# Where the constant rows of a decoder's running sums are written, and the order of four of its stages

## The chip, the cores and the metric

The kernel runs on one core of a Trainium2 chip, as one program and one launch. Its time is the device time of one execution in microseconds (us). The core has five engines that run independently: TensorE (PE, with its weight loads shown as PEld), VectorE (DVE), ScalarE (ACT), GpSimd (POOL) and SyncE (SP, which only issues transfers). Transfers (DMAs) are issued by SP, ACT and POOL and are moved by 16 DMA engines.

## What is computed

The reference is a decoder of four layers over 16 sequences of 128 tokens, 256 wide, in fp32. Each layer has an attention, a cross attention and a feed-forward part, every one followed by `x = _layernorm(x + part(x))`, so there are twelve stages in a chain, called s0 to s11 here. The change touches five of them:

- s0, a gated delta-rule attention. Its decays are products over time, computed as exponentials of differences of running sums.
- s3, a retention attention. Queries and keys are turned by position: `x * c + _rot(x) * s`, where `_rot` swaps neighbouring features. Then the scores `Q K^T` are multiplied with a decay matrix, and the output is normalised and gated.
- s1 and s2, a cross attention and a feed-forward part that is a table of splines, whose end is worked through together.
- s5, a gated feed-forward part with integer weights: `down(silu(gate(x)) * up(x))`, 704 hidden columns.
- s9, a state space layer (Mamba2) with 64 heads. The lines that matter:

```python
dt = jax.nn.softplus(dt + dt_bias)
A = -jnp.exp(A_log)
dA = jnp.transpose((dt * A).reshape(B_, nc, CS, NH), (0, 3, 1, 2))
A_cum = jnp.cumsum(dA, axis=-1)
Lmat = jnp.exp(_segsum(dA))
```

`_segsum` is the difference of two running sums for each pair of times.

## The kernel before, in words

The 16 sequences are worked as four groups (NG = 4) of four. `X` (tokens by features) and `xT` (its transpose) stay in SBUF for the whole run. A stage ends for a group with `finish_in_turns` (line 487): moments, normalisation, transposes into `xT`.

**Order of the work.** Stages are written as generators, and functions such as `rota` (line 290) take one step of each in turn. Where `self.nc` is an `Ordered` (line 320), compute instructions stay on their engine in the order in which they are written; nearly all instructions pass through there, so the profile shows them under line 332. Transfers on SP and parts that are not `Ordered` are placed by the framework's scheduler.

**Running sums (s0, s9).** The differences of running sums come out of a small matmul, 30 rows deep, whose two operands lie in one tile `up`. Its rows hold the sums, split in three parts and each part in a high and a low half, and constant rows of ones and selections. `sums` (line 402) makes DRAM tiles whose rows are filled from the constants, four heads at a time: it issues four transfers from DRAM to DRAM on ACT's queue, 256 KB each for s0 (`starts`) and 1024 KB each for s9 (`sums`). The kernel then overwrites the rows of the sums (for s0 at lines 663 and 664), and `load_sums` (line 413) reads a unit's rows into its `up`. s0's `sums` is called at line 594 in `w0`; s9's in `w7`, but it depends on nothing and is placed at the start of the run.

**The start.** SP loads `X`, `wab`, `w`, `sl`, `tbl` and the first weights, ACT loads constants. PE transposes `X` (line 476), ACT copies the transposes into `xT` (line 479). Slopes (`ss`, line 1097 and 1098) come from `sl`, and the gates of s0 from `wab`; from these come the sums `cums`, and with them stage s0 begins.

**s12_late** (line 1192) is the end of s1 and s2 with the first steps of s4's keys beside it. `s2_scores` marks for each token its bin (`oh`), and `turn(g)` transposes a group's marks on PE. All turns but the last come before the last call of `s2_scores`.

**s3.** `s3_turned` (line 1339) makes one half of a group's queries or keys: two projections, a copy `raw`, a transfer that swaps neighbouring rows (`sw`), two multiplications (`t` on POOL, `sw` on DVE) and their addition, on POOL. For keys ACT then writes two scaled copies `k`. `s3_unit` does the scores, decay (`ret` on DVE), normalisation (`var`, a power on POOL) and gating of a sequence.

**s5.** `s5_groups` (line 1828) goes through the groups one after the other: 48 matmuls for gate and up with ACT and DVE in between, then 48 matmuls for the down product, then `finish` of the group. The last group's `finish` is left to s6 (line 1911), where `first.insert(1, self.finish_in_turns(NG - 1))` puts it beside the first latents. In s4, `s5_prepare` (line 1778) prepares the integer weights step by step.

**s9.** Before its loop, `s9_sums` (line 2479) makes `dt`, `dA` and the sums of all four groups: 32 matmuls, softplus as Exp and Ln on ACT, the split in three parts on DVE, 48 matmuls with a triangle of ones, 24 transfers. `s9_group(0)` (line 2528) makes B and C of group 0. Then 64 units run (`s9_unit`, line 2564; four groups of 16), one step of each of the last units in every round of `rota`. A unit loads `wzx`, has 16 matmuls of 512 columns, 8 transposes (`xs`), 4 difference matmuls, 32 small ones (`y`) and 8 output matmuls (bankC). At its first step it takes one step of `more`; for units 8 to 15 of a group that is the next group's `s9_group`, for units 0 to 7 it is empty.

Of the kernel before, what the change touches and what calls it, by code (L numbers as in the profile page):

```python
# [22 lines left out]
S = 128  # L23
D = 256
NG = 4
# [309 lines left out]
class Decoder:  # L335
# [66 lines left out]
    def sums(self, heads, name):  # L402

        tiles = [self.dram.tile([heads, 32, S], F32, name=f"{name}_{g}") for g in range(NG)]
        lo = self.at["consts"]["up9"][0]
        for t in tiles:
            self.nc.scalar.dma_start(
                t.rearrange("(q i) r t -> q (i r) t", i=4),
                self.a["consts"][:, lo : lo + 128].unsqueeze(0).to_broadcast([heads // 4, 128, S]),
            )  # L410
        return tiles
# [173 lines left out]
    def w0(self, pool):  # L585
        nc = self.nc
        w = {}
        w["tri_le"] = self.const(pool, "tri_le", nc.scalar)
        w["tri_s"] = self.const(pool, "tri_s", nc.scalar)
        w["levels"] = self.const(pool, "levels", nc.scalar)  # L590
        w["ident32"] = self.const(pool, "ident32", nc.scalar)
        w["wab"] = pool.tile([128, 2, 32], F32, name="wab")
        nc.sync.dma_start(w["wab"], self.a["s0_wab"].rearrange("(k p) c -> p k c", p=128))
        self.starts0 = self.sums(16, "starts0")
        self.ends0 = [self.dram.tile([4, 16, 6, S], F32, name=f"ends0_{g}") for g in range(NG)]
        return w
# [595 lines left out]
    def s12_late(self, k12, wk, w, held, last):  # L1192
# [19 lines left out]
        for g in range(NG - 1):  # L1212
            turn(g)
        for _ in self.s2_scores(k12, held, NG - 1):
            next(keys, None)
        turn(NG - 1)
# [122 lines left out]
    def s3_turned(self, wk, w, g, part, qk):  # L1339
# [24 lines left out]
        if m == 0:  # L1364
            nc.gpsimd.tensor_tensor(q[:, c], t, sw, ALU.add)
        else:
            nc.gpsimd.tensor_tensor(t, t, sw, ALU.add)
            for par in range(2):
                nc.scalar.activation(kk[:, c, par], t, AF.Copy, scale=self.parity[:, par : par + 1])
# [391 lines left out]
    def w5(self, pool):  # L1761
# [10 lines left out]
        w["wide"] = pool.tile([128, 1], I32, name="wide5")  # L1772
        w["first"] = [
# [4 lines left out]
    def s5_prepare(self, w):  # L1778

        nc = self.nc  # L1780
        gur, wdr = w["gur"], w["wdr"]
        for k in range(2):
            for m in range(2):
                nc.gpsimd.tensor_scalar(gur[:, k, m, :704], w["gu_i"][:, k, m], 128.0, None, ALU.subtract)
                yield
# [42 lines left out]
    def s5_groups(self, wk, w, halves, last):  # L1828
# [12 lines left out]
        for g in range(NG):  # L1841
            if halves:
                hs = [wk.tile([128, 6, 512], F32R, tag="h5" + "hl"[n], name="h5" + "hl"[n]) for n in pair]
                gu, wd, xs = w["gur"], w["wdr"], halves[g]
            else:
                hs = [wk.tile([128, 6, 512], F32, tag="h5h", name="h5")]
                gu, wd, xs = w["gu"], w["wd"], [self.xT[:, :, 512 * g : 512 * g + 512]]
            of = len(xs)
            for c in range(6):
                n = 128 if c < 5 else 64  # L1850
                cols = slice(128 * c, 128 * c + (128 if halves else n))
                ps = []
                for m in pair:
                    p = self.ps(512)
                    for k in pair:
                        for i, x in enumerate(xs):
                            lhsT = gu[:, k, m, cols]
                            self.mm(p[: lhsT.shape[-1]], lhsT, x[:, k, :], of * k + i, 2 * of)
                    ps.append(p)
                t = wk.tile([128, 512], F32, tag="t5", name="t5")  # L1860
                nc.scalar.activation(t[:n], ps[0][:n], AF.Silu, scale=self.col("s5_sg")[:n, c : c + 1])
                h = wk.tile([128, 512], F32, tag="hf5", name="hf5", bufs=3) if halves else hs[0][:, c, :]
                nc.vector.scalar_tensor_tensor(
                    h[:n], ps[1][:n], self.col("s5_su")[:n, c : c + 1], t[:n], ALU.mult, ALU.mult
                )
                if halves:
                    nc.scalar.copy(hs[0][:n, c, :], h[:n])
                    nc.gpsimd.tensor_tensor(hs[1][:n, c, :], h[:n], hs[0][:n, c, :].bitcast(F32), ALU.subtract)
            if g == 0:
                self.load_transposed(NG - 1)  # L1870
            if halves and g + 2 < NG:
                halves.append(self.s5_halves(wk, g + 2))
            for half in pair:
                p = self.pt(2, D)
                for j in pair:
                    for c in range(6):
                        n = 128 if c < 5 else 64
                        lo = (2 * half + j) * 128
                        for i, h in enumerate(hs):
                            self.mm(p[:, j, :], h[:n, c, lo : lo + 128], wd[:n, c, :], of * c + i, of * 6)  # L1880
                t = wk.tile([128, 2, D], F32, tag="y5", name="y5")
                nc.vector.tensor_tensor(t, p, bc(self.row("s5_sd").unsqueeze(1), 128, 2, D), ALU.mult)
                xs_ = self.X[:, 4 * g + 2 * half : 4 * g + 2 * half + 2, :]
                nc.gpsimd.tensor_tensor(xs_, xs_, t, ALU.add)
            if last or g + 1 < NG:
                self.finish(g, last)

# [5 lines left out]
    def w6(self, pool):  # L1893
# [12 lines left out]
        w["vo"] = pool.tile([128, 8, D], F32, name="wvo6")  # L1906
        for t, src in zip((w["q"][:, :, 0, :], w["q2"][:64], w["vo"]), self.absorbed):
# [3 lines left out]
    def s6(self, wk, w, last):  # L1911
# [11 lines left out]
        first.insert(1, self.finish_in_turns(NG - 1))  # L1923
# [212 lines left out]
    def w7(self, pool):  # L2136
        self.sums9 = self.sums(64, "sums9")
# [309 lines left out]
    def s9(self, wk, w, last):  # L2447
# [12 lines left out]
        with (  # L2460
# [18 lines left out]
    def s9_sums(self, wk, w):  # L2479

        nc, pair = self.nc, range(2)
        dts = [w["dt"][:, 8 * k : 8 * k + 8, :] for k in pair]

        def twice(tag, bufs):
            return [wk.tile([128, 8, 64], F32, tag=tag, name=tag, bufs=bufs) for _ in pair]

        ea = wk.tile([128, 64], F32, tag="th9", name="ea9")
        nc.scalar.activation(ea, self.row("s9_al"), AF.Exp)
        for g in range(NG):
            gs = slice(4 * g, 4 * g + 4)  # L2490
            p = self.ps(4, 64)
            for j in range(4):
                for k in range(2):
                    self.mm(p[:, j, :], self.xTs(k, 4 * g + j), w["bcd"][:, k, 256:320], k, 2)
            nc.vector.tensor_tensor(
                w["dt"][:, gs, :], p, bc(self.row("s9_dtb").unsqueeze(1), 128, 4, 64), ALU.add
            )
        da = twice("sz9", 5)
        for d, t in zip(da, dts):
            nc.vector.scalar_tensor_tensor(d, t, -1.0, t, ALU.mult, ALU.min)  # L2500
        for d in da:
            nc.scalar.activation(d, d, AF.Exp)
        for d in da:
            nc.scalar.activation(d, d, AF.Ln, bias=1.0)
        parts = [twice("yx9", 2), twice("gT9", 2), da]
        for k in pair:
            d, t = da[k], dts[k]
            nc.vector.scalar_tensor_tensor(t, t, 0.0, d, ALU.max, ALU.add)
            nc.vector.scalar_tensor_tensor(d, t, -1.0, bc(ea.unsqueeze(1), 128, 8, 64), ALU.mult, ALU.mult)
        for n, unit in enumerate((2.0**-4, 2.0**-16)):  # L2510
            big = MAGIC * unit
            for k in pair:
                nc.vector.tensor_scalar(parts[n][k], da[k], big, big, ALU.add, ALU.subtract)
                nc.vector.tensor_tensor(da[k], da[k], parts[n][k], ALU.subtract)
        for g in range(2):
            for n in range(3):
                p = self.ps(4, 128)
                for j in range(4):
                    for k in pair:
                        self.mm(p[64 * k : 64 * k + 64, j, :], parts[n][k][:, 4 * g + j, :], w["tri_le"])  # L2520
                both = [wk.tile([128, 4, S], F32R, tag="m9", name="sum9", bufs=8) for _ in pair]
                self.halves(*both, p)
                for k in pair:
                    for hl in pair:
                        rows = self.sums9[2 * k + g][:, 10 * n + 5 * hl : 10 * n + 5 * hl + 4]
                        (nc.scalar, nc.gpsimd)[k].dma_start(rows, both[hl][64 * k : 64 * k + 64].bitcast(F32))
# [299 lines left out]
```

## Time and profile before

Three executions took 3757.82 us (median; 3754.70 and 3765.27 the others). The profile is of one more execution.

| | |
|---|---|
| the profiled execution's own time | 3764.13 us |
| its span, from the first to the last instruction | 3762.4 us |
| mean granted TensorE clock | 0.956 |
| PE busy | 3422.7 us, 91% of the span |
| DVE, ACT, POOL busy | 68%, 56%, 53% |

By time from the start of the span, the stages that matter lie so:

| stretch (us) | work | length (us) | PE busy (us) |
|---|---|---|---|
| 0 to 61 | start, gates and sums of s0 | 61 | 22.0 |
| 1387 to 1488 | s12_late | 101 | 74.4 |
| 1488 to 1640 | s3 | 152 | 126.8 |
| 1808 to 1905 | s5 | 97 | 86.4 |
| 2536 to 2607 | s9 ahead of its steady loop | 71 | 55.6 |
| 2607 to 3510 | the loop of s9 | 903 | 878.0 (some records are missing) |

In a line of the timeline the columns are: start, duration, engine, source line, operation, result and operands, their partitions and elements, how many of them; in brackets the engine's idle time before and what ended it. In a line of waits they are: the instruction that waited and its line, what it waited for; then the sum of the waits in us, how many, and the longest. Windows give per stretch the busy time of each engine (with the number of instructions), then the granted PE clock and the share and rate of the DMA engines.

### The profile page before, as it was taken

What the parts mean: (1) busy time and instruction counts of PE and PEld (TensorE: products, weight loads), DVE (VectorE), ACT (ScalarE), POOL (GpSimd) and SP (SyncE); (2) the same over time, 40 slices, a digit from 0 to 9 for tenths busy, and PEclk for the clock granted to TensorE, in tenths of its full rate; (3) what the DMA queues carried; (4) which work ended last, traced back from release to release, by engine and by line L of the source; (5) the groups of instructions that cost most, each with busy time, mean ns of one, the idle gap of its engine ahead of it and who ended that gap; (6) DMA issues with size and microseconds to landing.
All of it is one profiled execution on the core that took longest, in us unless ns stands there. A gap on an engine that the chain in (4) does not pass through costs nothing.

```text
span 3762.4 us, 95159 instructions
## 1 busy us (share of the span) xinstructions
PE 3422.7 (91%) x38821; PEld 2127.4 (57%) x38821; DVE 2547.4 (68%) x5495; ACT 2114.5 (56%) x4682; POOL 2012.6 (53%) x2313
## 2 busy tenths in 40 slices
PE   4899999999999987878889999988999999999896
PEld 3566666666666655656646665665455554555453
DVE  2677777767877756568444557756777777777797
ACT  2566666666666634345435445535666665666386
POOL 2344444444443434764455542345887676777467
PEclk8999999999999987978999998998999999999898
DMA  5111111111111115031100003112111111111220
GB/s 156 32 42 39 40 36 40 39 35 40 39 37 35 32 67 207 35 115 45 36 27 29 26 34 102 46 56 82 47 43 47 43 45 44 44 47 40 74 75 25
DMA packets 145271, 199.50 MB, mean 53 GB/s; under 512 B 14816, under 2 KB 98656, under 8 KB 141248
## 3 DMA queue, kind: packets, MB, share of 16 engines
q1 hardware_dynamic: 128912, 180.06, 14.9%
q10 hardware_dynamic: 14672, 9.03, 0.9%
q8 instruction: 310, 5.08, 0.5%
q0 software_dynamic: 1248, 4.28, 0.4%
q14 instruction: 129, 1.06, 0.1%
HBM read 159.49 MB, written 26.48 MB: 49 GB/s over the span
## 4 chain that ended last, share of the span: by engine, by line
PE 41%; DVE 9%; ACT 2%; POOL 2%; issue 2%; DMA 1%; SPq 0%; ACTq 0%; POOLq 0%; DVEq 0%
PE bankA L332 18%; PE bankB L332 15%; PE bankC L332 6%; DVE npad L332 2%; PE bankA L511 1%; PE bankB L511 1%; DVE y L332 1%; DVE acc L332 1%; DVE t L332 1%; DVE h L332 0%; DVE xp L332 0%; DVE X L332 0%; ACT L332 0%; DVE ln_st L332 0%; ACT e L332 0%
## 5 line engine op out<-in xcount | busy, mean ns | idle before, releaser
L332 PE MATMUL bankA<-xT,wzx 128*128 128x512 f32 x1024 | 458.5, 601 | 0.1
L332 DVE SCALAR_TENSOR_TENSOR acc<-bankA,half,acc 128x508 f32<-128x508 f32 (+2 forms) x384 | 285.3, 743 | 167.5 <-ACT acc L332 158.5
L332 PEld LDWEIGHTS bankA<-xT,wzx 128*128 128x128 f32 x1024 | 190.5, 191 | 226.4 <-issue 187.9
L332 POOL TENSOR_TENSOR m<-m,gm 128x512 f32<-128x512 f32 x252 | 312.8, 1275 | 9.8 <-ACT m L332 9.8
L332 PE MATMUL bankA<-xT,wkq 128*128 128x512 f32 x512 | 254.5, 621 | 0.4 <-ACT eb L332 0.2
L332 PE MATMUL bankA<-xT,wvg 128*128 128x512 f32 x512 | 251.7, 615 | 0.5 <-issue 0.5
L332 POOL TENSOR_TENSOR gT<-yx,sz 128x512 f32<-128x512 f32 x126 | 158.0, 1275 | 174.3 <-DVE yx L332 174.0
L332 POOL TENSOR_TENSOR eb<-eb,c_tri_s 128x512 f32<-128x512 f32 x64 | 81.2, 1268 | 299.2 <-ACT eb L332 299.2
L332 PE MATMUL bankC<-gT,wo 128*128 128x512 f32 x512 | 230.4, 593 | 1.5 <-DVE gT L332 1.5
L332 DVE TENSOR_REDUCE npad<-bankA 128x2 f32<-128x512 f32 (+1 forms) x320 | 197.2, 682 | 36.7 <-PE bankA L332 36.3
L332 ACT ACTIVATE m<-bankA 128x512 f32<-128x512 f32 x256 | 132.0, 603 | 129.2 <-PE bankA L332 129.2
L332 ACT ACTIVATE e<-bankA 128x512 f32<-128x512 f32 x320 | 164.9, 602 | 67.4 <-PE bankA L332 66.6
L332 POOL TENSOR_SCALAR rs_ve<-o_mv 128x4 f32<-128x4 f32 x64 | 31.6, 493 | 303.2 <-DVE o_mv L332 292.3
L332 POOL TENSOR_TENSOR sq<-sq,s 128x512 f32<-128x512 f32 x124 | 158.1, 1275 | 59.5 <-ACT s L332 54.8
L332 DVE SCALAR_TENSOR_TENSOR vT<-th,accv 128x512 f32<-128x512 f32 x64 | 45.8, 716 | 185.1 <-ACT th L332 185.1
L332 PEld LDWEIGHTS bankB<-y,tt 32*32 32x32 f32 x8192 | 86.8, 106 | 110.2 <-issue 76.2
L332 DVE SCALAR_TENSOR_TENSOR acck<-bankA,half_cols,acck 128x508 f32<-128x508 f32 (+2 forms) x192 | 142.5, 742 | 8.2 <-ACT acck L332 1.7
L332 PEld LDWEIGHTS bankC<-gT,wo 128*128 128x128 f32 x512 | 92.9, 190 | 96.4 <-issue 93.2
L332 ACT ACTIVATE acc<-bankA,half 128x512 f32<-128x512 f32 x128 | 100.6, 786 | 81.0 <-PE bankA L332 76.0
L332 DVE SCALAR_TENSOR_TENSOR accq<-bankA,half_cols,accq 128x508 f32<-128x508 f32 (+2 forms) x192 | 142.2, 741 | 4.5
L332 DVE SCALAR_TENSOR_TENSOR accv<-bankA,half_cols,accv 128x508 f32<-128x508 f32 (+2 forms) x192 | 140.1, 730 | 4.5
L332 ACT ACTIVATE m<-m 128x512 f32<-128x512 f32 x256 | 141.2, 650 | 0.0
(523 smaller groups left out, 9354.2 us busy)
## 6 DMA issues: line engine op xcount, KB each, us to landing
wzx<-in_s_wzx SPq DMA_DIRECT2D x64, 512.0 KB
wkq<-in_s_w SPq DMA_DIRECT2D x64, 256.0 KB
wvg<-in_s_w SPq DMA_DIRECT2D x64, 256.0 KB
wo<-in_s_wo SPq DMA_DIRECT2D x64, 128.0 KB
keys<-k SPq DMA_DIRECT2D x8, 1024.0 KB
k<-keys SPq DMA_DIRECT2D x8, 1024.0 KB
eo<-in_ctx_eo SPq DMA_DIRECT2D x32, 256.0 KB
e<-in_ctx_e SPq DMA_DIRECT2D x32, 256.0 KB
```

Of the source, the lines that this page charges most:

```text
L332: return lambda *a, **k: self.tc.keep_in_program_order(f(*a, **k))
L511: self.nc.tensor.matmul(out, lhsT=lhsT, rhs=rhs, start=(k == 0), stop=(k == n - 1))
```

## The change

It has these parts.

- `sums` writes its four tiles from a pattern in SBUF that `sums_first` loads (64 KB), and does so on SP. For s0 the pattern is loaded behind `wab`, and the four writes stand on SP behind `w` and ahead of `sl`, `tbl` and the first weights. For s9 the pattern is loaded in `w5` and the four writes are the first step of `s5_prepare`, during s4.
- In `s12_late` the turn of group 2 moves into the last call of `s2_scores`, behind its fourth step.
- In `s3_turned` the addition goes from POOL to DVE, for queries and for keys.
- `s5_groups` is cut in `s5_gates` and `s5_down`: the next group's gates stand ahead of a group's down product, and a group's `finish` is taken in two parts, the second behind the gates after that. The rest of the last `finish` goes to s6 as `self.ends`.
- `s9_sums` works for one group. Group 0's runs step by step beside `s9_group(0)` ahead of the loop, now in program order; those of groups 1 to 3 are steps of `more` for units 0 to 5 of the group before. Exp of `A_log` is taken once, ahead of it.

```diff
-    def sums(self, heads, name):
+    def sums_first(self, pool):
+        lo = self.at["consts"]["up9"][0]
+        first = pool.tile([128, 128], F32, name="sums_first")
+        self.nc.sync.dma_start(first, self.a["consts"][:, lo : lo + 128])
+        return first
+
+    def sums(self, first, heads, name):
         tiles = [self.dram.tile([heads, 32, S], F32, name=f"{name}_{g}") for g in range(NG)]
-        lo = self.at["consts"]["up9"][0]
         for t in tiles:
-            self.nc.scalar.dma_start(
-                t.rearrange("(q i) r t -> q (i r) t", i=4),
-                self.a["consts"][:, lo : lo + 128].unsqueeze(0).to_broadcast([heads // 4, 128, S]),
+            self.nc.sync.dma_start(
+                t.rearrange("(q i) r t -> (i r) q t", i=4), bc(first.unsqueeze(1), 128, heads // 4, 128)
             )
         return tiles
...
-        self.starts0 = self.sums(16, "starts0")
+        self.starts0 = self.sums(self.sums_first(pool), 16, "starts0")
...
-        for g in range(NG - 1):
+        for g in range(NG - 2):
             turn(g)
-        for _ in self.s2_scores(k12, held, NG - 1):
+        for n, _ in enumerate(self.s2_scores(k12, held, NG - 1)):
             next(keys, None)
+            if n == 3:
+                turn(NG - 2)
         turn(NG - 1)
...
-            nc.gpsimd.tensor_tensor(q[:, c], t, sw, ALU.add)
+            nc.vector.tensor_tensor(q[:, c], t, sw, ALU.add)
         else:
-            nc.gpsimd.tensor_tensor(t, t, sw, ALU.add)
+            nc.vector.tensor_tensor(t, t, sw, ALU.add)
...
+        w["sums"] = self.sums_first(pool)
...
+        self.sums9 = self.sums(w["sums"], 64, "sums9")
...
+        turned = {}
+        for g in range(NG + 1):
+            if g < NG:
+                turned[g] = self.s5_gates(wk, w, halves, g)
+                if g == 0:
+                    self.load_transposed(NG - 1)
             if halves and g + 2 < NG:
                 halves.append(self.s5_halves(wk, g + 2))
+            if g > 1:
+                for _ in ends:
+                    pass
+            if g:
+                self.s5_down(wk, w, halves, g - 1, turned.pop(g - 1))
+                ends = self.finish_in_turns(g - 1, last)
+                if last or g < NG:
+                    next(ends)
+        if last:
+            for _ in ends:
+                pass
+        else:
+            self.ends = [ends]
...
-        first.insert(1, self.finish_in_turns(NG - 1))
+        first.insert(1, self.ends[0])
...
-        self.sums9 = self.sums(64, "sums9")
...
-            self.s9_sums(wu, w)
-            for _ in self.s9_group(wu, w, 0):
+            ea = w["ea"] = wk.tile([128, 64], F32, name="ea9", **one)
+            nc.scalar.activation(ea, self.row("s9_al"), AF.Exp)
+            self.nc = Ordered(self.tc, nc)
+            for both in zip_longest(self.s9_sums(wu, w, 0), self.s9_group(wu, w, 0)):
                 pass
-            self.nc = Ordered(self.tc, nc)
...
-                    more, held = iter(()), {}
+                    more, held = self.s9_sums(wu, w, u // 16 + 1) if u < 48 else iter(()), {}
...
+    def s9_sums(self, wk, w, g):
+        nc = self.nc
+        t = w["dt"][:, 4 * g : 4 * g + 4, :]
+        d, part = [wk.tile([128, 4, 64], F32, tag=n, name=n, bufs=1) for n in ("da9", "part9")]
+        p = self.ps(4, 64)
+        for j in range(4):
+            for k in range(2):
+                self.mm(p[:, j, :], self.xTs(k, 4 * g + j), w["bcd"][:, k, 256:320], k, 2)
+        nc.vector.tensor_tensor(t, p, bc(self.row("s9_dtb").unsqueeze(1), 128, 4, 64), ALU.add)
+        nc.vector.scalar_tensor_tensor(d, t, -1.0, t, ALU.mult, ALU.min)
+        yield
+        nc.scalar.activation(d, d, AF.Exp)
+        nc.scalar.activation(d, d, AF.Ln, bias=1.0)
+        yield
+        nc.vector.scalar_tensor_tensor(t, t, 0.0, d, ALU.max, ALU.add)
+        nc.vector.scalar_tensor_tensor(d, t, -1.0, bc(w["ea"].unsqueeze(1), 128, 4, 64), ALU.mult, ALU.mult)
+        yield
+        for n in range(3):
+            src = d
+            if n < 2:
+                src, big = part, MAGIC * (2.0**-4, 2.0**-16)[n]
+                nc.vector.tensor_scalar(part, d, big, big, ALU.add, ALU.subtract)
+                nc.vector.tensor_tensor(d, d, part, ALU.subtract)
+            p = self.ps(4, 128)[:64]
             for j in range(4):
+                self.mm(p[:, j, :], src[:, j, :], w["tri_le"])
+            both = [wk.tile([64, 4, S], F32R, tag=f"sum9{m}", name="sum9", bufs=1) for m in range(2)]
+            self.halves(*both, p)
+            for m in range(2):
+                rows = self.sums9[g][:, 10 * n + 5 * m : 10 * n + 5 * m + 4]
+                nc.scalar.dma_start(rows, both[m].bitcast(F32))
+            yield
```

The bodies of `s5_gates` and `s5_down` are the two halves of the old `s5_groups`, unchanged. `w6` wraps its `nc` in `Ordered` ahead of three loads on SP, which `Ordered` passes through as they are.

More of the change, by code (lines that the diff above doesn't have):

```diff
@@ L1840, in s5_groups @@
             nc.gpsimd.tensor_scalar(wd[:64, 5, :], w["d_i"][:64, 5, :], 128.0, None, ALU.subtract)
[L1841 to L1870, printed above, removed]
@@ L1871, in s5_groups @@
+        turned = {}
[4 more added lines that the diff above has]
+                    self.load_transposed(NG - 1)
             if halves and g + 2 < NG:
                 halves.append(self.s5_halves(wk, g + 2))
[L1873 to L1884, printed above, removed]
@@ L1885, in s5_groups, with s5_operands @@
-            if last or g + 1 < NG:
-                self.finish(g, last)
+            if g > 1:
[11 more added lines that the diff above has]
+            self.ends = [ends]
+    def s5_operands(self, w, halves, g):
+        if halves:
+            return w["gur"], w["wdr"], halves[g]
+        return w["gu"], w["wd"], [self.xT[:, :, 512 * g : 512 * g + 512]]
@@ new lines, in s5_gates @@
+    def s5_gates(self, wk, w, halves, g):
+        nc = self.nc
+        pair = range(2)
+        if halves:
+            hs = [wk.tile([128, 6, 512], F32R, tag="h5" + "hl"[n], name="h5" + "hl"[n]) for n in pair]
+        else:
+            hs = [wk.tile([128, 6, 512], F32, tag="h5h", name="h5")]
+        gu, _, xs = self.s5_operands(w, halves, g)
+        of = len(xs)
+        for c in range(6):
+            n = 128 if c < 5 else 64
+            cols = slice(128 * c, 128 * c + (128 if halves else n))
+            ps = []
+            for m in pair:
+                p = self.ps(512)
+                for k in pair:
+                    for i, x in enumerate(xs):
+                        lhsT = gu[:, k, m, cols]
+                        self.mm(p[: lhsT.shape[-1]], lhsT, x[:, k, :], of * k + i, 2 * of)
+                ps.append(p)
+            t = wk.tile([128, 512], F32, tag="t5", name="t5")
+            nc.scalar.activation(t[:n], ps[0][:n], AF.Silu, scale=self.col("s5_sg")[:n, c : c + 1])
+            h = wk.tile([128, 512], F32, tag="hf5", name="hf5", bufs=3) if halves else hs[0][:, c, :]
+            nc.vector.scalar_tensor_tensor(
+                h[:n], ps[1][:n], self.col("s5_su")[:n, c : c + 1], t[:n], ALU.mult, ALU.mult
+            )
+            if halves:
+                nc.scalar.copy(hs[0][:n, c, :], h[:n])
+                nc.gpsimd.tensor_tensor(hs[1][:n, c, :], h[:n], hs[0][:n, c, :].bitcast(F32), ALU.subtract)
+        return hs
@@ new lines, in s5_down @@
+    def s5_down(self, wk, w, halves, g, hs):
+        nc = self.nc
+        pair = range(2)
+        of = len(hs)
+        _, wd, _ = self.s5_operands(w, halves, g)
+        for half in pair:
+            p = self.pt(2, D)
+            for j in pair:
+                for c in range(6):
+                    n = 128 if c < 5 else 64
+                    lo = (2 * half + j) * 128
+                    for i, h in enumerate(hs):
+                        self.mm(p[:, j, :], h[:n, c, lo : lo + 128], wd[:n, c, :], of * c + i, of * 6)
+            t = wk.tile([128, 2, D], F32, tag="y5", name="y5")
+            nc.vector.tensor_tensor(t, p, bc(self.row("s5_sd").unsqueeze(1), 128, 2, D), ALU.mult)
+            xs_ = self.X[:, 4 * g + 2 * half : 4 * g + 2 * half + 2, :]
+            nc.gpsimd.tensor_tensor(xs_, xs_, t, ALU.add)
@@ L1906, in w6 @@
         w["vo"] = pool.tile([128, 8, D], F32, name="wvo6")
+        nc = Ordered(self.tc, nc)
         for t, src in zip((w["q"][:, :, 0, :], w["q2"][:64], w["vo"]), self.absorbed):
@@ L2477, in s9 @@
             self.nc = nc
[L2479 to L2491, printed above, removed]
-            for j in range(4):
[L2493 to L2526, printed above, removed]
@@ new lines, in s9_sums @@
+    def s9_sums(self, wk, w, g):
+        nc = self.nc
+        t = w["dt"][:, 4 * g : 4 * g + 4, :]
[20 more added lines that the diff above has]
+            p = self.ps(4, 128)[:64]
+            for j in range(4):
+                self.mm(p[:, j, :], src[:, j, :], w["tri_le"])
[5 more added lines that the diff above has]
+            yield
```

## The prediction, made before the changed kernel had run

> **What bounds the kernel now.** I read the busy shares, then the timeline and the waits of the five stages that the change touches. All five edits matter only where PE waits, because PE is the bound nearly everywhere:
>
> ```profile
> PE 3422.7 (91%) x38821; PEld 2127.4 (57%) x38821; DVE 2547.4 (68%) x5495; ACT 2114.5 (56%) x4682; POOL 2012.6 (53%) x2313
> ```
>
> The start is the exception. In its timeline (PE, ACT, SP, DVE rows):
>
> ```profile
> 6.38 1.94 PE L476 MATMUL bankB<-c_ident,X 128*128 128x128 f32 x8 [6.38 <-DMA X<-in_x]
> 35.41 1.97 PE L476 MATMUL bankB<-c_ident,X 128*128 128x128 f32 x8 [27.09 <-ACT xT L479]
> ...
> 10.76 18.00 ACTq L407 DMA_DIRECT2D starts<-in_consts  x4
> 33.47 1.28 ACT L479 ACT_TABLE_LOAD   x1 [33.47 <-DMA c_cidx<-in_consts]
> ...
> 12.84 0.62 SPq L1088 DMA_DIRECT2D sl<-in_s_sl  x1
> ...
> 19.85 0.19 DVE L1097 TENSOR_REDUCE ss<-sl 128x2 f32<-128x32 f32 x1 [15.28 <-DMA sl<-in_s_sl]
> ```
>
> PE stands for 27.09 us because ACT, which must empty its banks, issues four transfers for 18 us and waits for the constants behind them.
>
> In s9's loop PE never waits; a unit takes 13.71 us. This is one round (PE rows, then DVE's):
>
> ```profile
> 2620.17 1.04 PE L332 MATMUL bankB<-c_ident,xs 128*128 128x128 f32 x8
> 2621.05 3.60 PE L332 MATMUL bankC<-gT,wo 128*128 128x512 f32 x8
> 2624.58 0.51 PE L332 MATMUL bankA<-up 30*128 30x512 f32 x4
> 2625.02 1.97 PE L332 MATMUL bankB<-m,xdt 128*64 128x128 f32 x32
> 2626.91 7.13 PE L332 MATMUL bankA<-xT,wzx 128*128 128x512 f32 x16
> ...
> 2622.28 1.28 DVE L332 TENSOR_TENSOR xdt<-bankB,dt 128x512 f32<-128x512 f32 x2
> ```
>
> Where a round has an extra piece, PE does wait: the piece stands behind the `xs` transposes and needs what DVE does after `xdt`. Its price is in this row: 1.81 us of waiting and 1.98 of work.
>
> ```profile
> 2677.85 1.98 PE L332 MATMUL bankB<-xT,bcd 128*128 128x512 f32 x4 [1.81 <-DVE xdt L332]
> ```
>
> The waits of PE in s12_late and s5, of all engines in s3, and of PE ahead of s9's loop:
>
> ```profile
> PE bankA L332 <- DVE oh L332: 7.1, 1, 7.1
> ...
> PE bankB L476 <- DVE X L494: 7.4, 3, 2.5
> ...
> ACT k L332 <- POOL t L332: 27.7, 7, 7.3
> ...
> PE bankB L511 <- DVE bcT L2538: 5.4, 1, 5.4
> PE bankA L511 <- DVE gT L2513: 4.7, 1, 4.7
> ```
>
> Last, the granted clock around an s5 stall of 2.51 us, and over the 1.81 us stall of s9. The first is followed by 3.4 us at half speed, the second by none:
>
> ```profile
> 1835.00:1838.40 3.40, 0.89 (x6) 0.43 (x4) 1.93 (x5) 0.83 (x2) 2.50 (x3) 1.00 0.00 0
> 1838.40:1841.90 3.50, 3.50 (x13) 2.81 (x12) 1.31 (x4) 2.02 (x4) 0.26 (x1) 0.51 0.00 0
> 2676.00:2679.50 3.50, 1.69 (x5) 0.87 (x5) 2.39 (x4) 0.84 (x2) 3.02 (x3) 1.00 0.50 150
> 2679.50:2683.00 3.50, 3.50 (x9) 1.33 (x7) 2.25 (x4) 1.81 (x3) 1.31 (x2) 1.00 0.00 0
> ```
>
> **The start: −9.5 us (−14 to +2).** ACT is free of the four `starts` issues and, among its copies, of the four `sums` issues, so it copies from about 14 us on and all transposes are over before 25. Then `sl` decides: the built order puts all transposes ahead of the slope matmuls, and these ahead of the `wab` ones, and on SP `sl` now stands behind the pattern's load and the four writes, the first of which waits until the pattern has landed. `sl` took 7.0 us from issue to use (12.84 to 19.85); so the pattern, issued at 12.3, lands near 19.3. An issue costs 0.5 us (SP's rows, 0.37 to 0.62) to 4.5 us (ACT's 18.00 for four). I take SP's, since most loads are over by then: 2 us for four. `sl` is issued at 21.5 and lands at 28.5. From there: 1.3 us for the slopes, 8.8 us for `wab` (3.13 + 1.87 + 3.76), and 13.0 us from the last `wab` matmul to the issue of `cums` (48.4 to 61.42), so 51.9 instead of 61.4. If `sl` lands with the transposes, near 24, the gain is 14; with ACT's issue times it lands near 44 and the start loses some 6, but then the two are unlikely to be equal, since the 4 MB of `sums` no longer share the engines; I stop the range at +2. What else SP delays (`tbl`, `wkq`, `wvg`, `wo`, `mask`, by 9 us) is needed after 50.
>
> **s4: 0 us.** The 4 MB of `sums` go out on SP during s4, where the page's slices have the DMA engines at 10 to 30%; the load of the pattern delays `k<-keys` by one issue, 0.5 us.
>
> **s12_late: −1.5 us (−7 to 0).** PE's wait of 7.1 us for `oh` goes, and the key projections behind it start earlier. But DVE sets the end there: `s2_scores` runs on it until 1441.9 and the table that follows needs it. What can shrink is DVE's slowing by POOL beside it (`xfsg` 2.20 us in the last call, 1.38 in others, two additions 3.34 against 2.44): 1.7 us.
>
> **s3: −5 us (−9 to +2).** Sixteen additions leave POOL (8 of 1.31, 8 of 1.27 us). On DVE each would take 0.68 (`ret`, the same size). The addition still waits for POOL's `t`, 1.72 us, and now `var`, `ret` and `yn` are queued behind that wait on DVE. For queries nothing is gained: PE's work of 7.23 us sets the round, and POOL comes to `var` no earlier than DVE will have it. For keys the copies `k` start 0.6 us earlier, and with them ACT's queue (`sq`, `gate`) on which PE waits: 8 × 0.6 = 5.
>
> DVE's `sw`, which reads two tiles in SBUF beside POOL's `t`, took 0.97 and 0.75 us, not 0.68. The Trainium skill has the rule, and it speaks against this part (GPSIMD Engine Reference, Specifications): GpSimd's SBUF interfaces are shared with VectorE, which contends with it through instructions with two SBUF inputs, as this addition is and `ret` is not. By that the part would be worth 8 × 0.3 = −2.4 instead of −5.
>
> **s5: −6.5 us (−10 to 0).** Gates take 48 × 0.233 = 11.2 us (the first 14.0, at a low clock), a down product 7.5. With the next gates ahead of it, `h5l` is ready (2.3 us of waits), and of the three waits of 2.5 us and their half-speed windows all go but one: the transposes of group 2 now stand behind the last down product's first matmuls and need that group's normalisation, about 6.5 us after its own down product, as from 1831.5 to 1838.2 before. Sum: 14.0 + 1.0 + 11.2 + 7.5 + 11.2 + 1.0 + 7.5 + 11.2 + 1.0 + 7.5 + 6.2 + 1.3 + 8.9 = 89.5 us, against 96.2 (1808.6 to 1904.8).
>
> **s9 ahead of the loop: −5 us (−10 to 0).** Half of the `bcd` matmuls (3.68 us), three quarters of the triangle's (of 8 us) and most of the two DVE waits leave. By the rows the first `wzx` comes at 2566 to 2568 instead of 2575.35. Group 1's Exp and Ln, with two table loads (0.4 + 1.28 + 0.4 + 1.28 = 3.3 us), now stand on ACT ahead of the first `th`, which PE waits for (1.1 us today), and give some 3 back.
>
> **s9's loop: +26 us (+8 to +30).** For each of groups 1 to 3, six units carry a piece:
> - the `bcd` matmuls: half of 3.68, 1.84 us of PE work (groups 2 and 3 only);
> - Exp and Ln, then two DVE operations: nothing, ACT is at 8.8 of 13.6 us and DVE at 10.0;
> - two pieces of `part` and four triangle matmuls. These stand on PE between the `xs` transposes (which end at 2621.21) and bankC, and need `part`, which stands on DVE behind `xdt` (2623.56) and takes 0.3: a wait of 2.75 us, and 0.6 of work (8 records at 0.08);
> - the third triangle product, 0.6 us, no wait.
>
> That is 3 × (2 × 3.35 + 0.6) + 2 × 1.84 = 25.6 us. PE has no slack in which it could go. Without any wait it would be 9.
>
> **The clock: +5 us (0 to +10).** Six new stalls of 2.75 us. A window of half speed costs 1.7 us of PE. Where idle time has to fill between 1.8 us (no drop) and 2.5 (a drop) of a 3.4 us window, a stall of 2.75 at a random place does so in some 78% to 34%: half of six, 3 × 1.7 = 5.
>
> The skill's rule (TensorE: Matmul & The Clock Gate, Part 1) is that the clock halves after an idle window of about 3.4 us. Read strictly no stall of 2.75 us is one and the term is 0; the s5 row, with PE busy for 0.89 of 3.40 us before the drop, says that less suffices.
>
> **Sum.** −9.5 + 0 − 1.5 − 5 − 6.5 − 5 + 26 + 5 = +3.5 us on the profiled execution's 3764.1, so 3767.6. That execution is 6.3 us above the median of the runs; carried over to it, 3761.3.
>
> **Rivals.**
> - *The stalls in s9 do not come about* (20%): DVE gets to `part` while PE still transposes. For it: DVE is idle for 3.7 us of a round. Against it: the 1.81 us row, where a piece in the same place did wait for `xdt`. The loop then costs 9 and the clock 0: 3.5 − 17 − 5 = −18.5, 3739.
> - *SP's queue holds back `sl`* (20%), the slower case: the four writes cost what ACT's did. For it: SP itself took 10.26 us for the four issues of `X` while the engines were full. Its price is each us by which `sl` lands after 28.5; at 36.5 the sum passes +11.3, and with the start at 0 the time is 3771.
> - *s3 and s5 give nothing* (10%): DVE's waits take back the keys' gain, and the last transposes of s5 cost what the three did. 3.5 + 11.5 = +15, 3773.
>
> **How the numbers follow.** My sum holds about as it is with 45%, 3750 to 3772. The last 5% are mishaps on either side. The measurement tells ±0.3%, 11.3 us, from no change. Faster is the first rival and half the mishaps, slower the other two; rounded, 0.24, 0.45 and 0.31. The range goes from the first rival's time to 3781, the sum of the slower ones short of both at once.
>
> **What would show it.** The first `xT` copy near 14 us and `cums` issued at 52 (right), or near 60 with SP's `starts` rows long (wrong). In s3 the wait of ACT's `k` for an addition gets shorter by 0.6 us a piece. In s5 one wait for `X` above 2.5 us, and 90 us in all. In the loop six PE rows of triangle matmuls with an idle time of 2.5 to 3 us ended by DVE `part`, rounds of 17.1 us; if that idle time is below 1, the forecast is wrong by its largest term.

## The result, and the profile after

The changed kernel takes 3778.46 us (median of eight executions, 3772.23 to 3788.74); the kernel before 3760.58 beside it (eight, 3750.29 to 3769.09). The ratio is 1.0051, with a 95% interval of 1.0033 to 1.0069: slower by 18 us, and by more than 0.3%. The time lies inside the range of the prediction, but on the side that had 0.31; the likeliest case was "no change".

The two profiled executions show less than the medians: 3772.23 after (the fastest of its eight) against 3764.13 before (above its median), 8.1 us. Among the eight after, the slowest also had the lowest granted clock (3788.74 us at a mean of 0.949, 3772.23 us at 0.954); executions of the kernel before do not order so (3748.33 and 3768.97 us, both at 0.960). So sizes of terms are read below from the profiles, and ratios carry the verdicts.

The difference between the two profiles, followed along the run by the same instruction in both (start after minus start before, in us; for the last output product of s3 its end):

| at | difference | what it says |
|---|---|---|
| first `wkq` matmul of s0 | −7.8 | the start |
| third unit of s0 (`vT`) | −14.7 | |
| first marks of s12_late (`oh`) | −21.2 | s0 is not changed; −6.5 |
| first projection of s3 (`wqk`) | −25.7 | s12_late, −4.5 |
| last output product of s3 | −26.6 | s3, −0.9 |
| first gate matmul of s5 | −27.0 | s4, −0.4 |
| first `sgu` matmul of s8 | −34.8 | s5, s6 and s7, −7.8 |
| last `sgu` matmul | −31.8 | s8, +3.0 |
| first `wzx` of s9's loop | −35.5 | s9 ahead of the loop, −3.7 |
| last `wzx` | +8.7 | s9's loop, +44.2 |
| last matmul | +8.0 | |

Everything up to the loop of s9 gained 35.5 us, more than the 27.5 forecast, and the loop then lost 44.2. Single rows of this table hold some chance: two profiles in which s12_late and s3 are as before (s9's pieces alone, and only s9's patterns moved, both below) differ from the profile of before by −3.7 us in the row of s12_late and by +2.7 in that of s3. The busy shares tell nothing of all this:

```profile
PE 3432.0 (91%) x38821; PEld 2130.8 (57%) x38821; DVE 2557.6 (68%) x5531; ACT 2126.9 (56%) x4698; POOL 1984.6 (53%) x2285
```

**The start.** The timeline of the changed kernel (PE, SP and DVE rows):

```profile
13.91 5.31 PE L481 MATMUL bankB<-c_ident,X 128*128 128x128 f32 x24 [5.96 <-ACT xT L484]
23.67 1.22 PE L516 MATMUL bankA<-c_ident,ss 128*128 128x128 f32 x4 [4.45 <-ACT ss L1103]
24.68 13.70 PE L516 MATMUL bankA<-wab,xT 128*128 128x32 f32 x64
...
17.00 2.79 SPq L413 DMA_DIRECT2D starts<-sums_first  x4
19.83 0.57 SPq L1093 DMA_DIRECT2D sl<-in_s_sl  x1
...
23.19 0.19 DVE L1102 TENSOR_REDUCE ss<-sl 128x2 f32<-128x32 f32 x1 [4.04 <-DMA sl<-in_s_sl]
```

The 27 us in which PE stood still are gone; it waits 4.45 us for `sl`. The four writes issue in 2.79 us on SP. But the `wab` products take 13.70 us where 8.8 were reckoned: the granted clock over 25.0 to 38.4 us is 0.50.

**A round of s9's loop with a split part** (PE), and the window behind its wait:

```profile
2574.22 1.04 PE L332 MATMUL bankB<-c_ident,xs 128*128 128x128 f32 x8
2578.13 1.27 PE L332 MATMUL bankA<-c_tri_le,part 128*64 128x128 f32 x8 [2.88 <-DVE part L332]
2579.34 5.13 PE L332 MATMUL bankC<-gT,wo 128*128 128x512 f32 x8
2584.40 0.50 PE L332 MATMUL bankA<-up 30*128 30x512 f32 x4
2584.83 1.97 PE L332 MATMUL bankB<-m,xdt 128*64 128x128 f32 x32
2586.73 7.13 PE L332 MATMUL bankA<-xT,wzx 128*128 128x512 f32 x16
...
2579.30:2582.70 3.40, 3.40 (x6) 1.58 (x6) 1.45 (x3) 1.73 (x3) 0.00 (x0) 0.57 0.35 77
```

PE waits 2.88 us for `part`, the triangle product takes over 1 us, and bankC, 3.60 us in a plain round, takes 5.13, because the clock stands at 0.57 in that window. From `wzx` to `wzx` this round is 19.48 us, the next one 19.92, the one with the third product 14.92, a plain one 13.71.

**Ahead of the loop and in its first rounds** (PE's waits from 2495 to 2562, then one row):

```profile
PE bankA L332 <- issue: 10.2, 1, 10.2
...
PE bankA L332 <- ACT m L332: 3.1, 1, 3.1
...
2552.60 9.98 PE L332 MATMUL bankA<-xT,wzx 128*128 128x512 f32 x16 [3.09 <-ACT m L332]
```

Ahead of the loop PE stands for 10.2 us before the first triangle product of group 0. In the loop Exp and Ln of group 1 with their table loads hold ACT up, PE waits 3.1 us for `m`, and the `wzx` behind it take 9.98 us instead of 7.13.

### The profile page after: what moved, and what is told of

It is laid out like the page before. It is cut to its first block, busy times and chain, and to the rows that moved or that the text cites. A ratio compares the mean times of both kernels' runs of the same rounds, so it can differ in the third digit from the quotient of the medians.

```text
span 3770.5 us, 95127 instructions
## 1 busy us (share of the span) xinstructions
PE 3432.0 (91%) x38821; PEld 2130.8 (57%) x38821; DVE 2557.6 (68%) x5531; ACT 2126.9 (56%) x4698; POOL 1984.6 (53%) x2285
## 4 chain that ended last, share of the span: by engine, by line
PE 70%; DVE 13%; ACT 8%; POOL 4%; issue 3%; DMA 2%; SPq 0%; ACTq 0%; POOLq 0%; DVEq 0%
PE bankA L332 40%; PE bankB L332 20%; PE bankC L332 8%; DVE npad L332 2%; PE bankA L516 2%; ACT accq L332 1%; ACT ot L332 1%; DVE X L332 1%; ACT gT L332 1%; DVE acc L332 1%; DVE accq L332 1%; PE bankB L516 1%; ACT L332 1%; DVE ln_st L332 1%; ACT eb L332 1%
## 5 line engine op out<-in xcount | busy, mean ns | idle before, releaser
L332 PE MATMUL bankC<-gT,wo 128*128 128x512 f32 x512 | 238.6, 610 | 1.5 <-DVE gT L332 1.5
```

Of the source, the lines that this page charges most:

```text
L332: return lambda *a, **k: self.tc.keep_in_program_order(f(*a, **k))
```

## The experiments

All times are medians, each ratio is to the kernel before, run beside it. The first three sections and the 9 transposes of the fourth ran together, so did the three sections after it, and last the 26 transposes and `sl` ahead.

### s9's sums put back ahead of the loop

```diff
-            for both in zip_longest(self.s9_sums(wu, w, 0), self.s9_group(wu, w, 0)):
+            self.s9_sums(wu, w)
+            for _ in self.s9_group(wu, w, 0):
                 pass
...
-                    more, held = self.s9_sums(wu, w, u // 16 + 1) if u < 48 else iter(()), {}
+                    more, held = iter(()), {}
```

> The changed kernel with s9's sums as they were (all four groups ahead of the loop); everything else changed. Theory A, the loss is the six stalls in s9's loop with the half-speed windows behind them, and the other parts gained: in the profiles the loop from the first xdt grew by 41.8 us and the stretch ahead of it shrank by 3.8, so this takes 3778 - 38 = 3740 us, about 20 to 30 below the kernel before. Rival B, the sums' matmuls are work that has to be paid in either place, and the loss is spread over the other parts: 3765 or more, no faster than before.

3735.35 us, ratio 0.9934 (0.9911 to 0.9958). It is faster than both kernels, by 25 us than before in the ratio and by 43 than the changed one. Its loop takes what the loop of before takes: first `wzx` at −28.2 us against before, last at −29.8. The loss is in s9 alone and theory A stands against B: the other parts are worth 0.66% together.

### s9's pieces alone

The kernel before, with the changed `s9` and `s9_sums` and nothing else.

> The kernel before with s9's sums as pieces of its units, nothing else. Theory A: 3760 + 38 = 3798 us, rounds of some 19.5 us where a part is split. Rival B: within 10 us of before.

3801.24 us, ratio 1.0111 (1.0090 to 1.0133), some 42 us slower. The loop is 44.5 us longer, as in the changed kernel (44.2). With two sections further down, the parts can be checked against the whole: pieces 1.0111, the start alone 0.9976 and the middle stages alone 0.9962 multiply to 1.0048; measured 1.0051.

### The split one round earlier

The splits of DVE move ahead by one step, into two tiles; the matmuls stay where they were.

```diff
+        parts = [part, wk.tile([128, 4, 64], F32, tag="part9b", name="part9b", bufs=1), d]
...
+        split(0)
         yield
         for n in range(3):
-            src = d
-            if n < 2:
-                src, big = part, MAGIC * (2.0**-4, 2.0**-16)[n]
-                nc.vector.tensor_scalar(part, d, big, big, ALU.add, ALU.subtract)
-                nc.vector.tensor_tensor(d, d, part, ALU.subtract)
+            src = parts[n]
+            if n == 0:
+                split(1)
```

`split(n)` holds the two removed DVE instructions.

> The changed kernel with each part split on DVE one round ahead of the matmuls that read it, in two tiles; same instructions, same matmuls at the same place in the round. Theory A: PE waits for no part any more, rounds with a triangle product take 13.7 + 0.6 to 0.7 us, not 19.5 and 19.9; six of them save 31, so 3747 us. Rival C, the matmuls themselves or the bank they need hold PE up there: rounds stay above 17 us and the time above 3768.

3749.63 us, ratio 0.9973 (0.9961 to 0.9985). The same two rounds (PE):

```profile
2580.62 1.04 PE L332 MATMUL bankB<-c_ident,xs 128*128 128x128 f32 x8
2581.59 1.09 PE L332 MATMUL bankA<-c_tri_le,part 128*64 128x128 f32 x8
2582.61 3.70 PE L332 MATMUL bankC<-gT,wo 128*128 128x512 f32 x8
...
2595.54 1.04 PE L332 MATMUL bankB<-c_ident,xs 128*128 128x128 f32 x8
2596.51 1.09 PE L332 MATMUL bankA<-c_tri_le,part9b 128*64 128x128 f32 x8
2597.53 3.70 PE L332 MATMUL bankC<-gT,wo 128*128 128x512 f32 x8
```

No wait, full clock, rounds of 14.9 us. Rival C falls: neither the matmuls nor a bank hold PE, the order does, with DVE's split standing behind `xdt` in the round in which PE needs it. The loop from the first `wzx` to the end of the last takes 926.0 us, against 954.2 in the changed kernel and 910.0 before. So 28.2 of the 44.2 us were the waits with what they do to the clock, and 16.0 stay: the products themselves, on an engine without slack, and some 3 us for the wait for `m` in the first rounds. That is why this kernel is still slower than the one with the sums ahead of the loop.

### PE kept busy in its wait

Needless transposes fill the time ahead of the split parts' products, in the rounds of groups 1 to 3; the products overwrite what they write. First 9 of them, then 26.

```diff
+            for j in range(9 if g and n < 2 else 0):
+                nc.tensor.transpose(p[:, j % 4, :], self.ident, self.ident)
```

> The changed kernel with 9 needless transposes on PE ahead of the triangle products of the two split parts (groups 1 to 3), where PE stands still for 2.9 to 3.3 us; they take some 2 us and write the bank that the products overwrite. Theory A, with the clock: the wait stays as long but PE is busy in it, the clock does not fall, bankC takes 3.6 us again instead of 5.1 to 5.4 and the rounds 17.2 to 17.6 instead of 19.5 and 19.9; about -12 us in all, 3766. Rival D, bankC is slow there for another reason (its banks, the weights): rounds as before or longer, 3778 or more.

3781.48 us, ratio 1.0065 (1.0044 to 1.0086): no gain. The 9 transposes took 1.15 us, less than reckoned, and left 1.81 to 2.29 us of waiting. In the rounds of group 1 the clock stayed full and they fell to 17.8 and 18.2 us, but in group 2 it fell again behind 2.29 us of waiting (PE rows, then the window):

```profile
2817.66 1.09 PE L332 MATMUL bankA<-c_tri_le,part 128*64 128x128 f32 x8 [2.29 <-DVE part L332]
2818.68 5.40 PE L332 MATMUL bankC<-gT,wo 128*128 128x512 f32 x8
...
2818.60:2822.00 3.40, 3.40 (x6) 1.47 (x5) 0.68 (x1) 1.73 (x3) 0.00 (x0) 0.52 0.36 77
```

That decides nothing between A and D, since the idle time was not gone. With 26:

> The changed kernel with 26 instead of 9 needless transposes ahead of the split parts' triangle products in s9's loop, so that PE is busy for all of its wait. Theory A, the clock falls because of the idle time: no window of half speed follows in any of the six rounds, bankC takes 3.6 to 3.7 us in all; the wait becomes work of about the same length, so the rounds lose the 1.7 us each that the half speed cost, 10 us in all less whatever the transposes take beyond the wait. Rival D: bankC stays above 5 us in most of the six rounds with PE busy ahead of it.

3772.55 us, ratio 1.0045 (1.0028 to 1.0062). Two rounds (PE), one row of a later round, and the window over the first product:

```profile
2573.59 3.00 PE L332 MATMUL bankA<-c_ident 128*128 128x128 f32 x26
2576.56 1.09 PE L332 MATMUL bankA<-c_tri_le,part 128*64 128x128 f32 x8
2577.57 3.70 PE L332 MATMUL bankC<-gT,wo 128*128 128x512 f32 x8
...
2594.74 1.09 PE L332 MATMUL bankA<-c_tri_le,part 128*64 128x128 f32 x8 [0.36 <-DVE part L332]
2595.76 3.70 PE L332 MATMUL bankC<-gT,wo 128*128 128x512 f32 x8
...
2826.75 3.58 PE L332 MATMUL bankB<-m,xdt 128*64 128x128 f32 x32 [1.31 <-DVE X L332]
...
2576.40:2579.80 3.40, 3.40 (x15) 1.90 (x14) 1.21 (x3) 0.87 (x2) 1.35 (x2) 1.00 0.12 27
```

PE is as late as ever, but busy. From the triangle product to the end of bankC the six rounds now take 4.7 us each, 28.3 in all, as in the kernel with the split one round earlier, which has no wait (28.3); in the changed kernel five of the six took 6.3 to 6.4, 36.4 in all. So the half speed behind these waits cost 8.1 us and idle time brought it: theory A, against D. One window of half speed is left in the six rounds, from 2826.7 to 2830.1 us: it lies behind bankC and another wait, of 1.31 us for `X` at the end of a group, and makes the `m` products take 3.58 us instead of 1.97. Theory A had forecast none. The loop is 6.8 us shorter than the changed kernel's; the intervals of the two ratios overlap, so for the time as a whole this is the profile's word.

### The start alone

The kernel before, with `sums_first`, `sums` and the two calls as in the change.

> The kernel before with only the sum patterns written from SBUF (s0's at the start, s9's during s4). Theory A: first wkq matmul at 52 instead of 60 us, third unit of s0 15 us earlier, so 3760 - 15 = 3745 us; s4 costs at most 2 us more. Rival E, what the start gives is given back along s0 or s4: 3755 or more.

3749.98 us, ratio 0.9976 (0.9964 to 0.9989), 9 us. Between what was expected here (15) and E's bound: the profile shows the first `wkq` 10.4 us earlier and the first marks of s12_late 17.2 us, but an execution with the start unchanged (s9's pieces alone) also moved by 5.1 us between the same two points. So some 5 of the −21.2 us in the table may be chance, and the 15 counted it as gain. The first `wkq` itself varies: with the start unchanged it came at 59.9, 62.0 and 67.6 us in three profiles, with the changed start at 49.0 to 52.2 in six.

### Only s9's patterns moved to s4

```diff
-        self.sums9 = self.sums(64, "sums9")
+        self.sums9 = self.sums(64, "sums9", nc.sync)
```

The new line stands in `s5_prepare`; the transfers stay DRAM to DRAM.

> The kernel before with only s9's 4 MB of pattern moved from the start to s4, still from DRAM to DRAM, on SP; s0's four writes stay on ACT. If the second 7 us that the start gained (between the first wkq matmul and the third unit) came from the 4 MB that no longer lie in front of s0's first loads: first wkq at 58 to 60, third unit some 7 us earlier, 3753 us. If they came from s0's own writes: third unit as before, 3760.

3764.13 us, ratio 1.0011 (1.0001 to 1.0022): neither case, no gain and by the interval a small loss; the first `wkq` comes 11.1 us later than in the profile of before. ACT's rows at the start:

```profile
10.57 21.18 ACTq L407 DMA_DIRECT2D starts<-in_consts  x4
31.79 5.92 ACTq L381 DMA_DIRECT2D c_cidx<-in_consts  x1
...
40.04 1.07 ACT L479 COPY xT<-bankB 128x512 f32<-128x512 f32 x2
```

With s0's four writes still on ACT its first copy comes at 40.04 us (34.77 before). So the 4 MB out of the way give nothing alone, and what the start gained lies in s0's own four writes, which no longer stand ahead of ACT's copies. Whether their move off ACT's queue or their source in SBUF counts for more was not tried apart.

### s12_late, s3 and s5 alone

The kernel before, with these three parts of the change.

> The kernel before with only the parts in s12_late, s3 and s5. Theory A: s12_late 3 to 8 us shorter, s3 3.4, s5 with the start of s6 7.8, so 3760 - 16 = 3744 us. Rival F, a good part of these differences between the two profiles was chance: 3755 or more.

3743.70 us, ratio 0.9962 (0.9944 to 0.9980), some 14 us: as expected, F falls. By its profile s12_late and s3 together gave 3.2 us (−3.4 and +0.2), s5, s6 and s7 8.3.

### sl ahead of the pattern's writes

The kernel of the first section, with s0's writes issued behind `sl` and `tbl`.

```diff
         nc.sync.dma_start(w["tbl"][:, :129], self.a["s2_tbl"])
+        self.starts0 = self.sums(self.starts_first, 16, "starts0")
```

> The fastest kernel so far (the changed one with s9's sums ahead of the loop, ratio 0.9934 to before), with s0's four pattern writes behind sl and tbl on SP instead of ahead of them. If the slopes' wait for sl is what holds PE between the last transposes (19.2 us) and the first slope matmul (23.7 us): sl is used near 20 us, the first wkq matmul comes 3 to 4 us earlier, ratio near 0.9925. If PE's clock at the start decides instead (the wab matmuls at half speed, 13.7 us): the slopes come earlier but wkq by less than 2.

3736.10 us, ratio 0.9944 (0.9926 to 0.9962), not to be told from the first section's 0.9934. In the profile (PE) the slopes come 2.7 us earlier than there (23.10), and so does the first `wkq` (46.4 against 49.0), between the two cases expected:

```profile
20.39 0.71 PE L516 MATMUL bankA<-c_ident,ss 128*128 128x128 f32 x4 [1.09 <-ACT ss L1104]
20.94 11.72 PE L516 MATMUL bankA<-wab,xT 128*128 128x32 f32 x64
```

The wait for `sl` was real and 3 us of it could be had; against the scatter of whole executions that is too little to measure.

## Why the prediction was right or wrong

The time fell inside the range, near its upper end, and the mechanism that decides was named in it: triangle products on PE behind `xs` and ahead of bankC, waiting for `part`. The forecast sum, 3761.3 us, was 17 us too low because of the sizes in the terms of s9's loop. That the range held owes something to its width: the 0.31 for slower stood mostly on two rivals, SP's queue and no gain in s3 and s5, and of these only the small gain of s3 came about.

- **s9's loop, +26, and the clock, +5: the steps that failed, by size.** Measured +44.2 between the first and the last `wzx`. The six waits are 2.88, 3.26, 3.36, 3.26, 3.36 and 3.26 us, 19.4 where 16.5 were reckoned (the terms given for the 2.75 us of one wait add up to 2.65). A triangle product adds 1.2 us to a round, not 0.6: its price came from the rows ahead of the loop, 0.08 us a record, where the matmuls alternate between the two halves of the columns, and here 8 records take 1.02 to 1.09 us. (That the alternating is the reason was not tried.) Nine of them make 5.4 us more than reckoned. The half speed followed five of the six waits, not half, and cost 8.1, not 5. And Exp and Ln at the loop's start, which the forecast had at 3 us in the term ahead of the loop, make the first two rounds 3.2 us longer (27.4 against 24.2). The kernel before had one window of half speed in its own loop, worth 1.5 us, which the profile after has not. That closes the account: 31 + 2.9 + 5.4 + 3.1 + 3.2 − 1.5 = 44.1.
- **The first rival, no waits in s9 (0.20).** It did not come about; the row of 1.81 us had it right. The kernel with the split one round earlier shows what it would have been: 3749.63, where the rival had 3739.
- **The start, −9.5: right in size, by errors that met.** Alone it measures 9 us (4 to 13 by the interval). `sl` was used at 23.2, not 28.5, because the pattern was in by 17.0 and not 19.3 and `sl` took 3.4 us and not 7.0; but `wab` took 13.7 us at half speed instead of 8.8. The term used durations of a stretch at a clock of 0.89, and these were one execution's: in the profile of s9's pieces alone, whose start is that of the kernel before, the same products took 5.17, 3.46 and 5.17 us, 13.8 in all. (The term's own parts add up to 51.6 us, not 51.9.) The second rival, SP's queue holding `sl` back (0.20), falls: four writes issued in 2.79 us.
- **s12_late, −1.5: not shown.** −3.3 to −4.8 us in six of the seven profiles that have the part, +0.1 in the seventh (s9's sums put back); but also −3.7 in two of the three other profiles without it, −0.2 in the third. Taken together with s3 it is clearer: −3.2 to −5.4 in six of the seven, +1.0 in the seventh, −1.0 to 0.0 in the three without. So the two parts are worth some 4 us together.
- **s3, −5: not gained (−0.9, and +0.2 alone).** Where s3 is unchanged this row reads +0.1 and twice +2.7, so a gain of some 2 us may hide in it; the 5 is not seen. The key rounds did get shorter, as forecast (7.24 us from score product to score product, 8.05 before), ACT waited 24.3 us instead of 27.7 for the additions ahead of `k`, and PE's wait for `gate` fell from 10.9 to 8.6. But early in the stage PE waited 2.8 us for `ret`, 0.3 before: there a query's addition now stands ahead of `ret` on DVE and took 1.56 us, not 0.68. (That it is the cause is read from the rows; no run tried it.) The waits of the changed kernel in s3, first of all engines, then PE's own, then the addition and the wait behind it:

```profile
POOL var L332 <- DVE var L332: 35.6, 13, 12.3
ACT k L332 <- DVE t L332: 24.3, 7, 8.1
...
PE bankB L332 <- ACT gate L332: 8.6, 3, 5.2
PE bankA L332 <- DVE ret L332: 2.8, 1, 2.8
...
1483.67 1.56 DVE L332 TENSOR_TENSOR q<-t,sw 128x512 f32<-128x512 f32 x1
...
1485.89 3.86 PE L332 MATMUL bankA<-q,k 32*128 32x128 f32 x32 [2.75 <-DVE ret L332]
```

  POOL's `var` waited 35.6 us instead of 14.7, but that is no loss: sixteen additions of 1.27 us and more left POOL, some 20 us in all. The rule of the Trainium skill on the shared SBUF interfaces (GPSIMD Engine Reference, Specifications) shows in the one addition that ran beside a POOL instruction, the one of 1.56 us above; the other fifteen took 0.69 us, with POOL standing still beside them.
- **s5, −6.5: right, and more.** From the first gate matmul to the end of the last down product it takes 87.0 us, 87.1 with the middle stages alone, against 96.2: −9.2 and −9.1 (with s6 and s7 behind it −7.8 and −8.3). The three waits for the normalisation became one, of 5.1 us (6.2 were reckoned), which explains 1.1 of the 2.5 us beyond the forecast; the rest is open. PE's waits from 1780 to 1890:

```profile
PE bankB L481 <- DVE X L499: 5.1, 1, 5.1
```

- **s9 ahead of the loop, −5 with ACT's delay in it.** −3.7 up to the first `wzx` (−3.7 to −6.4 in the five kernels with the part), where the forecast had −7 to −9, with ACT's delay, now counted in the loop, still to come: together some −0.5, not −5. What the term had wrong is that most of the DVE waits leave: the two of 5.4 and 4.7 us are gone, and one of 10.2 us stands in their place, ahead of group 0's first triangle product. In s8, which the change does not touch but for Exp of `A_log` being taken there, the profiles differ by +3.0 us (+2.2 to +3.1 in three other kernels with the pieces, −1.6 in a fourth, −2.3 to 0.0 in the five without); that is left open.
- **The clock's rule.** The Trainium skill (TensorE: Matmul & The Clock Gate, Part 1) has the clock halve after an idle window of about 3.4 us. The runs differ in this: waits of 2.2 to 3.4 us brought the half speed in most rounds, the plain 1.81 us waits in the loop none, and busy PE in the same place none. But the length of a wait does not decide alone, as the forecast had taken it: waits of 1.27 to 1.31 us for `X` at the end of a group brought the half speed in four of the eleven profiles, once in each. For a sum, the row of the trace was the better guide, and still too low. (The 78% in its working comes out at 75; that changes nothing.)
- **The median.** The forecast carried a sum made against one profile over to the median by their difference then, 6.3 us. By the parts measured alone the kernel is 0.48% slower, 18 us; the two profiles were 8 us apart by chance.

## What to carry to other kernels

Work that is moved out of a prelude into a loop is paid in full when the loop's bound engine has no slack, and if it waits there for another engine, it is paid more than twice: the matmuls themselves were some 15 us of the loss here, the waits 19 and the half-speed windows behind them 8. A piece for such a loop has to be split so that its producer runs a round ahead of its consumer. Before moving an operation to a faster engine, look at what stands behind it on the new queue; in s3 the rows suggest, though no run shows it alone, that this ate what the shorter duration saved. And read a term of a few us against more than one profile of the kernel before: here stretches whose code was the same differed by 3 to 8 us from profile to profile.

## What the runs showed of the hardware that was not expected

- Idle time of PE of 2.2 to 3.4 us in an otherwise full loop was followed by some 3.4 us at a clock of 0.52 to 0.57 in most rounds; with dummy transposes in the same gap the clock stayed at 1.00 there and the product and bankC together took 4.7 instead of 6.3 us. Waits of 1.27 to 1.31 us at the end of a group were followed by such a stretch in 4 of 33 cases, the 1.81 us waits of the same loop in none.
- PE can be busy and yet stay at half speed: 64 matmuls of 32 columns at the start ran for 13.7 us at 0.50 in the changed kernel, in 11.72 us at 0.59 in another one and, with transposes between them and other work ahead, at 0.89 in the kernel before. The order does not settle it: another execution with the start of before took 13.8 us for them, too.
- The issue of four transfers of 256 KB took 18.00 to 21.18 us on ACT from DRAM to DRAM, and 2.60 to 3.00 us on SP from SBUF; queue and source changed together, so the runs do not say which of the two matters.
